# The order of work in the slots of a selective scan, and what feeds and follows it: decays, dt's chain, gates, start values

## The chip, the cores and the metric

The kernel runs on one core of a Trainium2 chip, in float32. The metric is the device time of one execution in microseconds (us). A core has TensorE (PE, matmuls into the eight banks of PSUM), VectorE (DVE), ScalarE (ACT), GpSimd (POOL) and SyncE (SP, which here issues nearly all DMAs); each runs its own queue of instructions in order.

## The reference, cut to what matters

The network has four layers, each an attention-like block and a feed-forward block with a residual and a layer norm, on two sequences of 1024 tokens and 1024 channels. The change touches one block, the selective state space block of layer 2:

```python
def step(h, inp):
    x_t, dt_t, B_t, C_t = inp
    dA = jnp.exp(dt_t[..., None] * A)
    dBx = dt_t[..., None] * B_t[:, None, :] * x_t[..., None]
    h = dA * h + dBx
    y = jnp.einsum('bdn,bn->bd', h, C_t)
    return (h, y)
```

There are 2048 inner channels d and 16 states n. x is a projection of the input after a causal convolution of four taps and a silu; dt, B and C are projections of x, each normed, and dt goes through a second projection and a softplus. y gets D times x added, is multiplied by silu(z), where z is the second half of the input projection (the gate), and goes through an output projection.

## The kernel before, in words

`net_kernel` takes the two sequences one after the other; `l2_attn` computes the block for one of them. The 1024 tokens are two halves (u = 0, 1) of 512, the 2048 channels 16 chunks (c) of 128. A scan over 512 tokens is one VectorE instruction whose 128 partitions hold 8 channels times 16 states. So a half takes 256 scans, two to a slot: 128 slots (SL), 8 to a chunk, 256 slots for a sequence. The slot number k runs through both halves; `of(k)` gives half, chunk and place.

The order of everything in this stage is written out by hand in a loop over slots from k = -23 (BEFORE) to 261, inside `manual_schedule`. In a slot stand, in this order of issue:

- `rows(k + 6)` (L1273): SP loads dt times x for 8 channels, spread over the 16 states, from the DRAM tensor dxd into one of nine buffers h (512 KB);
- `times_b(k + 2)` (L1279): POOL multiplies h by B;
- `keep(k - 1)` (L1304): in u = 0, ScalarE copies the last column of the scans of the slot before into hst, from where the half u = 1 starts;
- one PE call of other work; then for m = 0, 1: `scan(k, m)` (L1296) on VectorE and `decay(k + 1, m)`: a PE matmul (L1286) that spreads dt from the tile hl into a PSUM bank, and ScalarE's exponential in place (L1288). In u = 1 `decay` also adds decay times hst into h's first column (L1291, a column operation of 128x1);
- between the two: the work that is due in this slot (`late`, filled by `at(k, f)`), and the second PE call;
- `states(k - 2)` in odd slots: PE sums over states into a bank py (L1316, L1318), one bank for a chunk;
- `times_c(k - 1)` (L1307): VectorE multiplies h by C, which lies in PSUM;
- in slots with k % 8 == 4: `y_out` is put down for eight slots later. It copies py with ScalarE (L1332), multiplies it by the gate with POOL (L1333), and stores it to yd (L1334).

The other PE calls are the projections of x for u = 1 (`ins`, with `l2_x` on ScalarE, `l2_taps` on VectorE, L1124, and `l2_silu` a slot apart each), of z (`gates`), of dt, B and C (`xproj`, then `l2_norm` and `l2_spread`), and the output projection of u = 0 (`outs`, L1441). All take their banks from one pool of eight (`ps`).

`l2_dt` starts a chunk's dt 16 slots before its first scan: a matmul, then ScalarE's softplus in pieces (`act1`, `act2`), sums and the product with x on POOL (`pool1`, `sum1`, `times_x`), four writes to dxd (L1240), the split of dt into hl and lo (`parts`, `rest`) and two transfers that put lo into hl (L1258; `send`). x comes back from the DRAM tensor xcd into xi (L1520). The steps' slots, counted from `l2_dt`, are given in a list:

```python
for n, f in ((1, act1), (2, act2), (3, pool1), (4, sum1), (5, times_x), (7, parts), (7, rest), (8, send)):
    at(k + n, f)
```

Of the kernel before, what the change touches and what calls it, by code (L numbers as in the profile page):

```python
# [27 lines left out]
class Net:  # L28
# [1032 lines left out]
    def l2_attn(self, b, ready, last):  # L1061
# [4 lines left out]
        with (  # L1066
# [56 lines left out]
                for k in range(1, 4):  # L1123
                    nc.vector.scalar_tensor_tensor(p, xp[:, k : k + HALF], cw[:, c, k : k + 1], p, ALU.mult, ALU.add)  # L1124

            def l2_silu(u, c, p):
                acc = tmp("xo")
                self.other = True
                nc.scalar.activation(acc, p, AF.Silu)
                nc.sync.dma_start(xcd[u][c][:], acc)  # L1130
                return acc

            def l2_px(u, c, acc):
# [24 lines left out]
                    elif c % 4 < 3:  # L1158
                        quarter[-1](c % 4 - 1)

            def l2_norm(u):

                raw = tmp("xo")
                nc.scalar.copy(raw[:NF, :], px.pop(u)[:NF, :])
                p = self.ps()
                for tt in range(4):
                    nc.tensor.transpose(
                        p[:, tt * NF : (tt + 1) * NF], raw[:NF, tt * P : (tt + 1) * P], self.ident[:NF, :NF]
                    )
                pn = tmp("pn", 1, 4 * NF)  # L1170
                nc.scalar.activation(pn, p[:, : 4 * NF], AF.Square)
                ss = self.small([P, 4, 3], "ss")
                parts = ((0, NR), (NR, N), (NR + N, N))
                pnv, pv = [t.rearrange("p (t f) -> p t f", f=NF) for t in (pn, p[:, : 4 * NF])]
                for j, (lo, n) in enumerate(parts):
                    nc.vector.tensor_reduce(ss[:, :, j], pnv[:, :, lo : lo + n], AX.X, ALU.add)
                nc.vector.tensor_scalar(ss[:, :, 0:1], ss[:, :, 0:1], 1.0 / NR, 1e-6, ALU.mult, ALU.add)
                nc.vector.tensor_scalar(ss[:, :, 1:3], ss[:, :, 1:3], 1.0 / N, 1e-6, ALU.mult, ALU.add)
                rr = self.small([P, 4, 3], "rr")
                self.rsqrt(rr, ss)  # L1180
                for tt in range(4):
                    for j, (lo, n) in enumerate(parts):
                        nc.vector.scalar_tensor_tensor(
                            pnv[:, tt, lo : lo + n], pv[:, tt, lo : lo + n], rr[:, tt, j : j + 1],
                            lnw[:, lo : lo + n], ALU.mult, ALU.mult,
                        )
                return pnv
# [20 lines left out]
            def l2_dt(u, c, k):  # L1208

                p = self.ps()  # L1210
                nc.tensor.matmul(
                    p, wd[c // 8][: NF + 1, (c % 8) * P : (c % 8 + 1) * P], norms[u][0], start=True, stop=True
                )
                xs[u, c] = xc = tmp("xi")
                at(k + 3, nc.sync.dma_start, xc, xcd[u][c][:])
                e, one, lg = tmp("e", 1), tmp("one", 1), tmp("lg", 1)
                dt, dtx = lg, e
                rl = tmp("rl", 1)

                def act1():  # L1220
                    nc.scalar.activation(rl, p, AF.Relu)
                    nc.scalar.activation(e, p, AF.Abs)
                    nc.scalar.activation(e, e, AF.Exp, scale=-1.0)

                def act2():
                    nc.scalar.activation(one, e, AF.Identity, bias=self.one)
                    nc.scalar.activation(lg, one, AF.Ln)
                    nc.scalar.activation(one, one, AF.Identity, bias=neg)

                def pool1():  # L1230
                    nc.gpsimd.tensor_tensor(e, e, one, ALU.subtract)
                    nc.gpsimd.tensor_tensor(lg, lg, e, ALU.add)

                def sum1():
                    nc.gpsimd.tensor_tensor(dt, lg, rl, ALU.add)

                def times_x():
                    nc.gpsimd.tensor_tensor(dtx, dt, xc, ALU.mult)
                    for j in range(4):
                        nc.sync.dma_start(dxd[u][c][:, j, :], dtx[32 * j : 32 * j + 32, :])  # L1240

                low = [None]

                def parts():

                    hl[u, c] = tp.tile([P, 2, HALF], R, tag="hl", bufs=2, name=self.nm("hl"))
                    nc.scalar.copy(hl[u, c], dt.unsqueeze(1).to_broadcast([P, 2, HALF]))

                def rest():

                    lo = low[0] = tp.tile([P, HALF], R, tag="lo", bufs=1, name=self.nm("lo"))
                    nc.gpsimd.tensor_tensor(lo, dt, hl[u, c][:, 0, :].bitcast(F), ALU.subtract)

                def send():

                    lo = low[0]
                    for j in range(2):
                        nc.sync.dma_start(  # L1258
                            hl[u, c][64 - 64 * j : P - 64 * j, j, :].bitcast(F), lo[64 * j : 64 * j + 64, :].bitcast(F)
                        )  # L1260

                for n, f in ((1, act1), (2, act2), (3, pool1), (4, sum1), (5, times_x), (7, parts), (7, rest), (8, send)):
                    at(k + n, f)


# [17 lines left out]
            def decay(k, m):  # L1283
                u, c, q, jj = of(k)
                dA[k, m] = self.ps()
                nc.tensor.matmul(dA[k, m], rep[:, 4 * m + q, :], hl[u, c][:, jj, :], start=True, stop=True)  # L1286
                g = 16 * c + 4 * q + 2 * jj + m
                nc.scalar.activation(dA[k, m], dA[k, m], AF.Exp, scale=A[:, g : g + 1])  # L1288
                if u:
                    h0 = hs[k][:, m, 0:1]  # L1290
                    nc.scalar.activation(h0, dA[k, m][:, 0:1], AF.Identity, scale=hst[:, g : g + 1], bias=h0)  # L1291

            def scan(k, m):
                u, c, q, jj = of(k)
                g = 16 * c + 4 * q + 2 * jj + m
                nc.vector.tensor_tensor_scan(  # L1296
                    hs[k][:, m, :], dA.pop((k, m)), hs[k][:, m, :], 0.0, ALU.mult, ALU.add
                )

            def keep(k):  # L1300
# [27 lines left out]
            def y_out(k):  # L1328
                u, c = k // SL, k % SL // 8
                sz = zt.pop((u, c))  # L1330
                yo = tmp("one", 1)
                nc.scalar.copy(yo, py.pop((u, c)))  # L1332
                nc.gpsimd.tensor_tensor(sz, sz, yo, ALU.mult)  # L1333
                nc.sync.dma_start(yd[u][c][:], sz)  # L1334

            def ins(u):

                def one(u, c):
# [6 lines left out]
                    def call(k, now):  # L1345
                        if k == 0:
                            w["p"] = self.ps()
                        p = w["p"]
                        nc.tensor.matmul(  # L1349
                            p, w["w"][:, k * P : (k + 1) * P], self.xcols(k, u0, HALF), start=k == 0, stop=k == KD - 1  # L1350
                        )
                        if k == KD - 1:
                            def x():
                                w["x"] = l2_x(u, c, p)
                            at(now + 1, x)
                            at(now + 2, lambda: l2_taps(c, p, w["x"]))

                            def s():
                                w["s"] = l2_silu(u, c, p)
                                silu_z()  # L1360
                            at(now + 3, s)
                    return load, [(call, k) for k in range(KD)]
# [2 lines left out]
            def xproj(u):  # L1365

                def one(c2):
# [7 lines left out]
                    def call(n, now):  # L1375
                        l2_px(u, 2 * c2 + n, w["x"][:, n * HALF : (n + 1) * HALF])
                        if 2 * c2 + n == NCH - 1:
                            at(now + 1, lambda: at(now + 3, l2_spread, u, l2_norm(u)))
                    return load, [(call, n) for n in range(2)]
                return [one(c2) for c2 in range(NCH // 2)]  # L1380

# [80 lines left out]
            with self.tc.manual_schedule():  # L1462
# [12 lines left out]
                take(xproj(1), 4)  # L1475
                take(z0[12:] + z1[:6], 20)
                taken = 0
                at(-BEFORE, lambda: at(4 - BEFORE, l2_spread, 0, l2_norm(0)))
                for k in range(-BEFORE, 2 * SL + 6):
                    if -16 <= k < 2 * SL - 16 and k % 8 == 0:  # L1480
                        l2_dt((k + 16) // SL, (k + 16) % SL // 8, k)
# [26 lines left out]
                        times_b(k + 2)  # L1508
                    if 0 <= k - 1 < 2 * SL:
                        keep(k - 1)  # L1510
                    pe()
                    for m in range(2):
                        if live:
                            scan(k, m)
                        if 0 <= k + 1 < 2 * SL:
                            decay(k + 1, m)
                        if m:
                            break
                        for f, args in late.pop(k, []):
                            f(*args)  # L1520
                        pe(True)
                    if k % 2 == 1 and 0 <= k - 2 < 2 * SL:
                        states(k - 2)
                    if 0 <= k - 1 < 2 * SL:
                        times_c(k - 1)
                    if live and k % 8 == 4:
                        at(k + 8, y_out, k)
                    if live and k % 8 == 0:
                        skip(k // SL, k % SL // 8)
                while late:  # L1530
# [462 lines left out]
```

## Time and profile before

| | |
|---|---|
| time, median of 3 runs | 5128.9 us (5122.4 to 5136.8) |
| the profiled execution's own time | 5130.3 us |
| its span, first to last instruction | 5128.4 us |
| granted TensorE clock, mean | 0.968 |
| busy share PE, DVE, ACT, POOL | 92%, 61%, 41%, 41% |
| scans L1296 | 1024, 1207 ns each |
| products with C, L1307 | 512, 1193 ns each |
| products with B, L1279 (POOL) | 512, 2367 ns each |
| exponentials L1288 (ACT) | 1024, 657 ns each |
| column operations L1291 (ACT) | 512, 352 ns each |
| first and last scan, first sequence | 1052.1 to 2003.4 us |
| first and last scan, second sequence | 3601.9 to 4545.4 us |

The profile is of one execution. A row of a group gives line, engine, operation, output<-inputs, sizes, count, then busy time and the mean of one in ns, then the time that the engine sat idle before it and who ended that. Row "DVE h L1296 <- ACT h L1291" of the waits reads: VectorE sat idle before L1296 until ScalarE's L1291 was done; the numbers are us in all, times, longest. In a table by stretch each engine has its busy time and, in brackets, its instructions; PEclk is the granted clock, DMA share the mean busy share of the 16 DMA engines.

### The profile page before, as it was taken

Reading aid. Unit: us, or ns where it says so; the run is one execution under the profiler, and the core shown is the slowest. Engines: PE = TensorE matmul, PEld = TensorE weight load, DVE = VectorE, ACT = ScalarE, POOL = GpSimd, SP = SyncE. Lnnn points to the kernel's source line nnn. Section 1 sums busy time; section 2 is a strip of 40 time slices with the busy share of each in tenths; the row PEclk is TensorE's granted clock in tenths of the full one; section 3 lists DMA queues with packets and bytes.
Section 4 is the critical chain, followed back from the end, with each engine's and each line's share of the span. In section 5 each row is a group of like instructions: output and inputs, shape, how many; then the busy total and the mean of one; then the engine's idle time right before and its main releaser. Section 6 shows DMA issues by size and latency. Waiting matters only on the chain. (4 is left out here: it accounts for less than half of the span.)

```text
span 5128.4 us, 50257 instructions
## 1 busy us (share of the span) xinstructions
PE 4706.3 (92%) x16584; PEld 2237.2 (44%) x16584; DVE 3128.0 (61%) x4322; ACT 2109.7 (41%) x4485; POOL 2097.7 (41%) x1259
## 2 busy tenths in 40 slices
PE   8989989998897888999999999899888988899999
PEld 3347645433332333455433576554333333344544
DVE  5453256389999997225365422652899999963153
ACT  2431232377677774001024311424776777720010
POOL 2013121078798885100020220200887998831010
PEclk9999999999999999999999999999999999999999
DMA  2144212388889998201111432113888899971100
GB/s 88 36 159 143 97 48 81 131 216 217 220 225 242 236 244 226 90 33 46 49 67 38 173 119 89 54 51 103 220 219 224 214 247 245 249 210 65 55 20 33
DMA packets 254871, 708.06 MB, mean 138 GB/s; under 512 B 37008, under 2 KB 54544, under 8 KB 254612
## 3 DMA queue, kind: packets, MB, share of 16 engines
q1 hardware_dynamic: 248340, 683.88, 46.7%
q0 software_dynamic: 6272, 20.98, 1.2%
q8 instruction: 133, 2.18, 0.2%
q14 instruction: 126, 1.03, 0.1%
HBM read 599.60 MB, written 86.25 MB: 134 GB/s over the span
## 5 line engine op out<-in xcount | busy, mean ns | idle before, releaser
L1296 DVE TENSOR_TENSOR_SCAN h<-ps,h 128x512 f32<-128x512 f32 x1024 | 1204.1, 1207 | 88.9 <-ACT h L1291 47.2
L1279 POOL TENSOR_TENSOR h<-h,br 128x1024 f32<-128x1024 f32 x512 | 1201.0, 2367 | 43.3 <-DMA h<-dxd 20.7
L1286 PE MATMUL ps<-hl,rep 128*128 128x512 f32 x1024 | 717.9, 708 | 119.9 <-DVE h L1296 94.7
L1288 ACT ACTIVATE ps<-ps,l_Alog 128x512 f32<-128x512 f32 x1024 | 667.9, 657 | 216.9 <-PE ps L1286 213.6
L1307 DVE TENSOR_TENSOR h<-h,ps 128x1024 f32<-128x1024 f32 x512 | 610.8, 1193 | 0.0
L1403 PE MATMUL ps<-xT,w 128*128 128x512 f32 x1024 | 541.1, 615 | 10.2 <-DVE h L1296 7.9
L1608 POOL TENSOR_TENSOR x<-x,row 128x1024 f32<-128x1024 f32 x48 | 112.3, 2349 | 796.0 <-PE ps L130 796.0
L1286 PEld LDWEIGHTS ps<-hl,rep 128*128 128x128 f32 x1024 | 198.6, 195 | 523.6 <-DVE h L1296 340.1
L152 DVE TENSOR_TENSOR x<-x,ps 128x512 f32<-128x512 f32 x192 | 128.4, 681 | 434.4 <-PE ps L1785 145.6
L1318 PE MATMUL ps<-h,sel 128*32 128x512 f32 x2048 | 365.1, 638 | 18.8 <-DVE h L1307 18.2
L104 PE MATMUL ps<-xT,w 128*128 128x512 f32 x768 | 336.1, 592 | 0.0
L177 ACT ACTIVATE rs<-mv 128x1 f32<-128x1 f32 (+2 forms) x88 | 17.9, 203 | 705.7 <-DVE mv L171 705.4
L1441 PE MATMUL ps<-w,w 128*128 128x512 f32 x512 | 279.9, 630 | 20.8 <-DMA w<-yd 12.1
L1403 PEld LDWEIGHTS ps<-xT,w 128*128 128x128 f32 x1024 | 190.6, 195 | 204.2 <-issue 136.7
L104 PE MATMUL ps<-w,xT 128*128 128x512 f32 (+1 forms) x768 | 278.3, 522 | 0.0
L1124 DVE SCALAR_TENSOR_TENSOR ps<-xp,l_convw,ps 128x512 f32<-128x512 f32 x192 | 144.4, 752 | 213.4 <-ACT ps L1119 208.9
L767 POOL TENSOR_TENSOR s<-s,l1r 128x512 f32<-128x512 f32 x64 | 66.5, 1040 | 487.7 <-DVE l1r L766 481.8
L1349 PE MATMUL ps<-xT,w 128*128 128x512 f32 x512 | 251.9, 602 | 0.7
L1291 ACT ACTIVATE h<-ps,h,hst 128x1 f32<-128x1 f32 x512 | 180.0, 352 | 118.5 <-POOL h L1279 93.9
L1782 PE MATMUL ps<-w,xT 128*128 128x512 f32 x512 | 227.4, 597 | 0.0
L1622 PE MATMUL ps<-w,w 128*128 128x512 f32 x512 | 222.6, 594 | 4.2 <-DMA w<-yd 4.2
L104 PEld LDWEIGHTS ps<-xT,w 128*128 128x128 f32 x768 | 144.8, 189 | 183.4 <-issue 177.6
(289 smaller groups left out, 7319.9 us busy)
## 6 DMA issues: line engine op xcount, KB each, us to landing
h<-dxd SPq DMA_DIRECT2D x512, 512.0 KB, 7.2
w<-l_in SPq DMA_DIRECT2D x128, 512.0 KB, 6.7
w<-l_out SPq DMA_DIRECT2D x96, 512.0 KB, 6.2
w<-l_conv SPq DMA_DIRECT2D x54, 512.0 KB, 3.9
w<-cvd SPq DMA_DIRECT2D x36, 512.0 KB, 3.3
w<-l_fw SPq DMA_DIRECT2D x32, 512.0 KB, 4.4
xcd<-xo SPq DMA_DIRECT2D x64, 256.0 KB, 2.2
xi<-xcd SPq DMA_DIRECT2D x64, 256.0 KB, 5.4
```

The costliest lines, as they stand in the source:

```text
L104: self.nc.tensor.matmul(out, lhsT, rhs, start=j == 0, stop=j == n - 1)
L1279: nc.gpsimd.tensor_tensor(hs[k], hs[k], norms[of(k)[0]][1].unsqueeze(1).to_broadcast([P, 2, HALF]), ALU.mult)
L1286: nc.tensor.matmul(dA[k, m], rep[:, 4 * m + q, :], hl[u, c][:, jj, :], start=True, stop=True)
L1288: nc.scalar.activation(dA[k, m], dA[k, m], AF.Exp, scale=A[:, g : g + 1])
L1296: nc.vector.tensor_tensor_scan(hs[k][:, m, :], dA.pop((k, m)), hs[k][:, m, :], 0.0, ALU.mult, ALU.add)
L1307: nc.vector.tensor_tensor(hs[k], hs[k], norms[of(k)[0]][3].unsqueeze(1).to_broadcast([P, 2, HALF]), ALU.mult)
L1318: nc.tensor.matmul(py[u, c][32 * j : 32 * j + 32, :], self.sel[:, q, :], hs[k - 1 + j // 2][:, j % 2, :], start=False, stop=q == 3,)
L1349: nc.tensor.matmul(p, w["w"][:, k * P : (k + 1) * P], self.xcols(k, u0, HALF), start=k == 0, stop=k == KD - 1)
L1403: nc.tensor.matmul(p, w["w"][:, k * P : (k + 1) * P], self.xcols(k, u * HALF, HALF), start=k == 0, stop=k == KD - 1)
L1441: nc.tensor.matmul(p, y[:, cc, t * P : (t + 1) * P], wt[:, cc * HALF : (cc + 1) * HALF], start=c2 == 0 and cc == 0, stop=last,)
L1622: nc.tensor.matmul(acc[tt], y[:, cc * HALF + tt * P : cc * HALF + (tt + 1) * P], w[:, cc * HALF : (cc + 1) * HALF], start=c == 0, stop=c = ...
L1782: nc.tensor.matmul(p, self.xcols(k, tt * P, P), wt[k][:, ns], start=k == 0, stop=False)
```

## The change

- The due work of a slot (`late`) comes ahead of the first PE call and of both scans.
- After `scan(k, 0)` comes `decay(k + 1, 1)`, after `scan(k, 1)` comes `decay(k + 2, 0)`: each decay stands one scan sooner in the order.
- The column operation is gone from `decay`; `scan` takes its initial value from hst in u = 1.
- `y_out` comes six slots after it is put down, not eight, and multiplies on VectorE, straight from py; the store to yd is issued a slot later.
- dt's chain has one step of an engine in a slot and is longer; the product with x uses the tile `one`, not `e`; the writes to dxd and the product with x are apart.
- `l2_silu` of u = 1 stores its result a slot later. `l2_norm` is cut in two, a slot apart, and `l2_spread` comes a slot later for u = 1.

```diff
-            def l2_silu(u, c, p):
+            def l2_silu(u, c, p, now=0):
...
-                nc.sync.dma_start(xcd[u][c][:], acc)
+                if u:
+                    at(now + 1, nc.sync.dma_start, xcd[u][c][:], acc)
+                else:
+                    nc.sync.dma_start(xcd[u][c][:], acc)
...
-            def l2_norm(u):
+            def l2_norm1(u):
...
                 nc.scalar.activation(pn, p[:, : 4 * NF], AF.Square)
+                return p, pn
+
+            def l2_norm(u, p, pn):
...
-                at(k + 3, nc.sync.dma_start, xc, xcd[u][c][:])
+                at(k + 4, nc.sync.dma_start, xc, xcd[u][c][:])
...
-                dt, dtx = lg, e
+                dt, dtx = lg, one
...
                 def act1():
                     nc.scalar.activation(rl, p, AF.Relu)
                     nc.scalar.activation(e, p, AF.Abs)
+
+                def act2():
                     nc.scalar.activation(e, e, AF.Exp, scale=-1.0)
 
-                def act2():
+                def act3():
                     nc.scalar.activation(one, e, AF.Identity, bias=self.one)
+
+                def act4():
                     nc.scalar.activation(lg, one, AF.Ln)
+
+                def act5():
                     nc.scalar.activation(one, one, AF.Identity, bias=neg)
 
                 def pool1():
                     nc.gpsimd.tensor_tensor(e, e, one, ALU.subtract)
+
+                def pool2():
                     nc.gpsimd.tensor_tensor(lg, lg, e, ALU.add)
...
                 def times_x():
                     nc.gpsimd.tensor_tensor(dtx, dt, xc, ALU.mult)
+
+                def send_x():
                     for j in range(4):
                         nc.sync.dma_start(dxd[u][c][:, j, :], dtx[32 * j : 32 * j + 32, :])
...
-                for n, f in ((1, act1), (2, act2), (3, pool1), (4, sum1), (5, times_x), (7, parts), (7, rest), (8, send)):
+                for n, f in (
+                    (1, act1), (2, act2), (3, act3), (4, act4), (5, act5), (5, pool1), (6, pool2), (7, sum1),
+                    (8, times_x), (8, parts), (9, send_x), (9, rest), (10, send),
+                ):
                     at(k + n, f)
...
                 nc.scalar.activation(dA[k, m], dA[k, m], AF.Exp, scale=A[:, g : g + 1])
-                if u:
-                    h0 = hs[k][:, m, 0:1]
-                    nc.scalar.activation(h0, dA[k, m][:, 0:1], AF.Identity, scale=hst[:, g : g + 1], bias=h0)
...
-                    hs[k][:, m, :], dA.pop((k, m)), hs[k][:, m, :], 0.0, ALU.mult, ALU.add
+                    hs[k][:, m, :], dA.pop((k, m)), hs[k][:, m, :], hst[:, g : g + 1] if u else 0.0, ALU.mult, ALU.add
...
                 sz = zt.pop((u, c))
-                yo = tmp("one", 1)
-                nc.scalar.copy(yo, py.pop((u, c)))
-                nc.gpsimd.tensor_tensor(sz, sz, yo, ALU.mult)
-                nc.sync.dma_start(yd[u][c][:], sz)
+                nc.vector.tensor_tensor(sz, sz, py.pop((u, c)), ALU.mult)
+                at(k + 7, nc.sync.dma_start, yd[u][c][:], sz)
...
                     if 0 <= k - 1 < 2 * SL:
                         keep(k - 1)
+                    for f, args in late.pop(k, []):
+                        f(*args)
                     pe()
                     for m in range(2):
                         if live:
                             scan(k, m)
-                        if 0 <= k + 1 < 2 * SL:
-                            decay(k + 1, m)
+                        if 0 <= k + 1 + m < 2 * SL:
+                            decay(k + 1 + m, 1 - m)
                         if m:
                             break
-                        for f, args in late.pop(k, []):
-                            f(*args)
                         pe(True)
...
                     if live and k % 8 == 4:
-                        at(k + 8, y_out, k)
+                        at(k + 6, y_out, k)
```

More of the change, by code (lines that the diff above doesn't have):

```diff
@@ L1358, in s @@
                             def s():
-                                w["s"] = l2_silu(u, c, p)
+                                w["s"] = l2_silu(u, c, p, now + 3)
                                 silu_z()
@@ L1377, in call @@
                         if 2 * c2 + n == NCH - 1:
-                            at(now + 1, lambda: at(now + 3, l2_spread, u, l2_norm(u)))
+                            at(now + 1, lambda: w.update(n=l2_norm1(u)))
+                            at(now + 2, lambda: at(now + 4, l2_spread, u, l2_norm(u, *w["n"])))
                     return load, [(call, n) for n in range(2)]
@@ L1477, in l2_attn @@
                 taken = 0
-                at(-BEFORE, lambda: at(4 - BEFORE, l2_spread, 0, l2_norm(0)))
+                at(-BEFORE, lambda: at(4 - BEFORE, l2_spread, 0, l2_norm(0, *l2_norm1(0))))
                 for k in range(-BEFORE, 2 * SL + 6):
```

## The prediction

> **What bounds the kernel now.** I read the page first (slices, groups), then busy time by stretch, then what VectorE waits for in each stretch, then single slots. The scans are two stages, slices 8 to 15 and 28 to 35, one for each sequence. I cut each at the slot where its second half (u = 1) begins.
>
> ```profile
> span 5128.4 us, 50257 instructions
> ...
> DVE  5453256389999997225365422652899999963153
> ...
> POOL 2013121078798885100020220200887998831010
> ```
>
> ```profile
> core 0: us, PE busy (x) PEld busy (x) DVE busy (x) ACT busy (x) POOL busy (x), PEclk, DMA share, GB/s
> 1052.00:1536.40 484.40, 428.78 (x1341) 162.80 (x1339) 462.92 (x438) 345.03 (x659) 418.91 (x226) 0.97 0.84 220
> 1536.40:2003.40 467.00, 395.33 (x1241) 147.64 (x1239) 440.18 (x398) 339.46 (x674) 399.58 (x212) 0.95 0.93 240
> 3601.80:4084.20 482.40, 429.21 (x1342) 163.18 (x1340) 463.10 (x437) 345.00 (x659) 419.04 (x226) 0.97 0.83 220
> 4084.20:4545.50 461.30, 395.99 (x1240) 146.71 (x1238) 439.69 (x398) 339.56 (x674) 399.70 (x212) 0.95 0.93 244
> ```
>
> VectorE is busy 94 to 96% of all four stretches; no other compute engine is. So a scan stage lasts as long as VectorE's work plus VectorE's idle time: 21.5 + 26.8 + 19.3 + 21.6 = 89 us in all. That is the most the change can save inside the stages. Who causes it, from the waits of VectorE in the first sequence's stage:
>
> ```profile
> engine line waited for: us in total, times, longest us
> DVE h L1296 <- ACT h L1291: 26.1, 33, 2.3
> DVE h L1296 <- ACT ps L1288: 13.2, 14, 2.3
> ```
>
> The first is all of u = 1, the second all in u = 0; the second sequence has 21.1 and 18.1. Both are ScalarE being late: with the exponential of a decay (L1288), or with the column operation behind it (L1291). An undisturbed slot is two scans and one product:
>
> ```profile
> 1440.01 2.33 DVE L1296 TENSOR_TENSOR_SCAN h<-ps,h 128x512 f32<-128x512 f32 x2
> 1442.25 1.19 DVE L1307 TENSOR_TENSOR h<-h,ps 128x1024 f32<-128x1024 f32 x1
> 1443.37 2.33 DVE L1296 TENSOR_TENSOR_SCAN h<-ps,h 128x512 f32<-128x512 f32 x2
> ```
>
> It takes 3.36 us, though the three durations (1.207 twice, 1.193) add to 3.61: each instruction starts 82 ns before the one ahead ends. So an added VectorE instruction costs its duration less about 0.08 us.
>
> **The change, part by part.**
>
> *Gate on VectorE.* Removed, 64 times: ScalarE's copy L1332 (0.58 us) and POOL's product L1333 (1.27). Added, 64 times: one VectorE product of an SBUF and a PSUM operand. Nearest row is L982, the same form: 685 ns, 605 net. 62 lie inside the scans, where nothing covers them: **+37 us**. On POOL eight slots cost 8 x 2.37 + 6 x 1.27 = 26.6 us before, against VectorE's 26.9; after, 25.3.
>
> *No column operation.* Removed, 512 times: L1291 on ScalarE (352 ns, 180 us in all), which also made ScalarE wait for POOL's product (93.9 us over the run). Added: the scan of u = 1 takes its initial value from a column of hst. No row shows a scan with one. Rows of like shape with and without a per-partition scalar:
>
> ```profile
> L1723 DVE SCALAR_TENSOR_TENSOR x<-ps,rinv,x 128x512 f32<-128x512 f32 x32 | 22.9, 746 | 9.0 <-PE ps L104 8.7 <-issue 0.3
> ...
> L628 DVE SCALAR_TENSOR_TENSOR qkv<-cf,ps 128x512 f32<-128x512 f32 x22 | 15.1, 686 | 69.4 <-PE ps L612 69.4
> ```
>
> 60 ns more. Bounds: nothing, if the scan loads its start under other work, and 66 ns (L1124 against L628); a gain is excluded, since the form only adds a read. I take 60: 512 x 0.06 = **+31 us**.
>
> A rule speaks against this part. Rows inside the scans:
>
> ```profile
> L1124 DVE SCALAR_TENSOR_TENSOR ps<-xp,l_convw,ps 128x512 f32<-128x512 f32 x33 | 24.6, 747 | 2.0 <-ACT ps L1119 1.2
> ...
> L181 DVE TENSOR_TENSOR rsq<-rsq,ss 128x12 f32<-128x12 f32 x1 | 2.3, 2261 | 0.0
> ```
>
> L181, tiny, takes 2261 ns here. The Trainium skill (SBUF — State Buffer, "Who interferes with whom") says why: a VectorE instruction with two SBUF inputs shares a read port with GpSimd, and one waits out the other. If the column counted as a second SBUF input beside h, each of the 512 scans could wait about 1 us (half a POOL product): some +500 us. But L1124 reads xp and its scalar from SBUF, and keeps 747 ns with POOL at 86%. I take the row: no lock. The gate reads one SBUF and one PSUM operand, as L982.
>
> *Decays half a slot sooner, due work first.* No instruction added. Decay n is now issued after scan n-3 instead of n-2, and ScalarE does a slot's due work before both exponentials instead of between them. Check on a stall of before: in slots 12, 28, ... ScalarE runs, from the end of a scan, keep 0.19, exp 0.66, gate copy 0.58, table load 1.28, silus 0.60 + 2 x 0.62, table load 1.28, exp 0.66 = 6.5 us; the second exp is due after 1.12 + 3.36 + 1.13 = 5.6. Short by 0.9; the trace has 1.11 at five slots. After: keep 0.19, Ln 0.63, the same 4.4, exp 0.66 = 5.9: short by 0.3. An extra PSUM bank is held by decays; the gate, read at slot 10 of a chunk instead of 12, gives one back before the next accumulator is taken. Counting tiles in program order, a decay's bank was freed 3 to 4 scans earlier before, 4 to 5 after.
>
> *dt's chain.* Same instructions, one ScalarE or POOL step a slot. It goes from step 5 to step 9 for the four dxd writes, 8 to 10 for the two hl writes, 3 to 4 for the xi load; the y write goes a slot after its product, and the xcd writes of u = 1 a slot after the silu. All go through SP; POOL issues no DMA in these stages. SP no longer stands waiting for POOL (L1240 85.1 us, L1334 73.6 in the first sequence), and POOL no longer for xi (17.1). Several u = 1 stalls (1.97 and 2.28 us at chunk starts) go back to that late xi load. What tightens is the dxd write against the first row load (a rival below).
>
> *Sum.* Idle 89 us goes. What is late next: in u = 0 the silu slot (5 x 0.4), the norm and the start, about 4.5 a sequence; in u = 1 row loads and out-projection weights at a DMA share of 0.93, about 5.5; so 20 us remain. Before and after the stages: the first decay one half slot sooner in PE's queue, and the last gate without its 1.86 us of copy and POOL product, about -3 a sequence. -89 + 20 + 37 + 31 - 6 = **-7 us** on the profiled execution's 5130.3 (span 5128.4). That execution is 1.4 above the median, 5128.9, of the three runs; on the median the sum gives 5122, and I say 5124, as PE's wait at the gate (next) is not quite nothing.
>
> Bounds of the gate's own wait: the product stands first in VectorE's queue at slot 10 and needs PE's last state sums of slot 9, and both scans are queued behind it. In the trace those sums end mostly 0.6 to 2.2 us before that slot, and twice after it; they move behind one more decay. Zero to 1.1 us (one scan) each: 0 to 70 us. I take 2 in all, since the decay's bank is free four scans back.
>
> **The rivals.**
>
> *The scan's start is free.* For: a scan takes 1133 ns from start to start, against 605 for a product of as many elements, so one more read may hide in it. Against: both scalar forms pay. 5124 - 31 = 5093.
>
> *Slack not bought.* ScalarE's late work is as long as before; if half of the 89 us stays, 5124 + 24 = 5148. Against: ScalarE loses 108 us of work per sequence.
>
> *The row loads come late (slower).* Before, dxd was written five steps before the first row load of its chunk. Now it is one. SP comes to the write in an odd slot, behind a row load that waits for that slot's state sums (2.4 us), issues four (1.7), and the next row load stands in SP until they land (median 2.9, longest 9.4). It goes 7 us into slot 9 instead of 2. Then landing (median 8.5 in u = 1, longest 14.3) and POOL's 2.4: 18 of the 24.4 us to its scan. Cover is 6 us at the medians; it decides when both landings together pass 17.5 us, against 11.4. hl, queued behind, lands at about 17. If half of the 32 chunks of u = 1 lose 2.3 us, +37: 5161. For it: DMA share 0.93. Against: the total traffic is the same, and SP's other waits go.
>
> **How the numbers follow.** Main case 0.46, 5124, own range 5106 to 5142. Free start 0.22; slack not bought 0.15; late rows 0.17. Within 0.3% (15 us), which is about what a measurement of this kernel can tell from no change, lie most of the main case and a third of the slack case. Faster: 0.25 of the main case and nearly all of the free start, 0.33. Slower: nearly all of the late rows, two thirds of the slack case, a little of the main, 0.27. Same: 0.40. The range runs from the free start with all stalls gone (5086) to the late rows (5163).
>
> **What would show it.** Right: VectorE's waits in the scans about 20 us in all, no L1291; 64 gate products near 0.68 us and with hardly a wait; scans of u = 1 near 1.27 us, those of u = 0 unchanged; u = 0 stretches 6 to 10 us shorter, u = 1 within 8 us of before. Wrong: u = 1 scans at 1.21 (then 5093); waits of POOL's product on h<-dxd in every chunk, or SP's L1273 on dxd for over 5 us each (then 5161); gate products that wait for PE.

## The result: 0.8% slower, and the profile after

The changed kernel takes 5170.0 us (median of 4 runs, 5165.4 to 5173.5) where the kernel before takes 5129.6 in the same comparison: a ratio of 1.0081, with a 95% interval of 1.0065 to 1.0097. The profiled execution has a span of 5164.2 us, 35.8 more than before. The prediction was 5124, with a range that ended at 5163: it was wrong, in sign and in size.

First the slices of the page after: nothing has changed its bound. VectorE is the full engine of slices 8 to 15 and 28 to 35, as before.

```profile
span 5164.2 us, 49160 instructions
...
DVE  5452266389999997215365422652999999962153
...
POOL 2023020078797874100010320201887978731010
```

Then the table by stretch, cut at the same places (first scan, first scan of u = 1, last scan, for each sequence).

```profile
core 0: us, PE busy (x) PEld busy (x) DVE busy (x) ACT busy (x) POOL busy (x), PEclk, DMA share, GB/s
1054.80:1532.30 477.50, 422.29 (x1333) 161.88 (x1332) 465.97 (x450) 329.21 (x637) 396.11 (x209) 0.96 0.83 219
1532.30:2012.90 480.60, 402.32 (x1238) 145.91 (x1238) 462.30 (x414) 251.53 (x402) 381.24 (x198) 0.93 0.88 238
3618.20:4099.00 480.80, 422.46 (x1333) 162.57 (x1332) 465.50 (x451) 329.29 (x637) 396.00 (x209) 0.96 0.83 217
4099.00:4583.00 484.00, 404.33 (x1238) 146.53 (x1238) 462.41 (x414) 251.22 (x402) 381.38 (x198) 0.92 0.88 236
```

The stretches of u = 0 are 6.9 and 1.6 us shorter than before, those of u = 1 are 13.6 and 22.7 us longer. In all the stages grew by 28 us: VectorE's work by 50.3, while its idle time (length less busy) fell from 89.0 to 66.7, so by 22.3 only. The remaining 7.9 us lie outside the stages. There, each first scan stands 4.2 us farther behind its norm than before (66.0 us instead of 61.8), because the taps (L1124) of slot 0, and the ScalarE step that they wait for, are now ahead of it:

```profile
1052.58 2.34 DVE L1124 SCALAR_TENSOR_TENSOR ps<-xp,l_convw,ps 128x512 f32<-128x512 f32 x3 [7.67 <-ACT ps L1119]
...
1054.83 3.45 DVE L1313 TENSOR_TENSOR_SCAN h<-ps,h 128x512 f32<-128x512 f32 x3
```

What each instruction costs is as predicted. Three rows of the page's groups: scans of u = 1, scans of u = 0, POOL's product with B; then two of the gate products by tile (shortest, median and longest in ns; `row` and `zo` are two places in which z is kept).

```profile
L1313 DVE TENSOR_TENSOR_SCAN h<-ps,hst,h 128x512 f32<-128x512 f32 x512 | 628.9, 1267 | 26.1 <-ACT ps L1308 26.1
L1313 DVE TENSOR_TENSOR_SCAN h<-ps,h 128x512 f32<-128x512 f32 x512 | 598.5, 1207 | 14.9 <-ACT ps L1308 14.9
L1299 POOL TENSOR_TENSOR h<-h,br 128x1024 f32<-128x1024 f32 x512 | 1205.1, 2368 | 131.7 <-DMA h<-dxd 91.0
```

```profile
L1348 DVE TENSOR_TENSOR row<-row,ps x32: 676/681/690, 1088.4 to 4534.1; 128x512 f32<-128x512 f32 x32
L1348 DVE TENSOR_TENSOR zo<-zo,ps x32: 669/686/689, 1148.3 to 4588.1; 128x512 f32<-128x512 f32 x32
```

The scan with a start value costs 60 ns more, the gate product 0.68 us. What is not as predicted is in the waits. The lines of VectorE and ScalarE in the first sequence's stage (total us, times, longest):

```profile
engine line waited for: us in total, times, longest us
ACT ps L1308 <- PE ps L1306: 212.9, 227, 4.3
...
ACT one L1235 <- DMA dxd<-one: 99.5, 29, 10.2
...
DVE h L1313 <- ACT ps L1308: 17.2, 15, 5.6
...
DVE zo L1348 <- PE ps L1335: 6.5, 9, 1.2
...
DVE row L1348 <- PE ps L1335: 3.8, 3, 2.0
```

Two kinds are new. ScalarE stands 29 times, for 99.5 us, at L1235 (`act3`, 1 + e) until a DMA has *read* the tile `one`: the trace of before shows no such wait of ScalarE. And VectorE waits 12 times at the gate for PE's state sums; over both stages the gate's waits are 19.2 us, and scans wait 41.0 us for an exponential (L1308).

One of the long waits, from the timeline (start, duration, engine and line, idle before it in brackets; lines between left out):

```profile
1630.74 3.77 SPq L1257 DMA_DIRECT2D dxd<-one  x4
...
1640.30 0.72 ACT L1235 ACTIVATE one<-e,one 128x512 f32<-128x512 f32 x1 [10.18 <-DMA dxd<-one]
...
1640.92 1.22 ACT L1308 ACTIVATE ps<-ps,l_Alog 128x512 f32<-128x512 f32 x2
1641.60 1.28 DVE L1313 TENSOR_TENSOR_SCAN h<-ps,hst,h 128x512 f32<-128x512 f32 x1 [5.63 <-ACT ps L1308]
```

The four writes of dt times x to dxd are issued from 1630.7 us on; ScalarE may overwrite `one` for the next chunk only when they have landed, at 1640.3. The exponentials of two decays stand behind it in ScalarE's queue, and the scan that needs the first is 5.63 us late.

It follows from the list of steps. dt times x now lives in `one`, of which there is one buffer. It is written to dxd at step 9, and the next chunk, eight slots behind, writes `one` at its step 3, which is step 11: two slots, 6.7 us at 3.36 us a slot, for an issue and a landing that here took 9.6. Before, dt times x lived in `e`, written to dxd at step 5 and overwritten by the next chunk at step 9: four slots, 13.4 us, and ScalarE did not wait for it.

### The profile page after: what moved, and what is told of

The parts are those of the page before. It is cut to its first block, busy times and chain, and to the rows that moved or that the text cites. A ratio compares the mean times of both kernels' runs of the same rounds, so it can differ in the third digit from the quotient of the medians.

```text
span 5164.2 us, 49160 instructions
## 1 busy us (share of the span) xinstructions
PE 4712.2 (91%) x16584; PEld 2233.8 (43%) x16584; DVE 3180.9 (62%) x4386; ACT 1908.1 (37%) x3909; POOL 2017.0 (39%) x1195
## 5 line engine op out<-in xcount | busy, mean ns | idle before, releaser
L1306 PE MATMUL ps<-hl,rep 128*128 128x512 f32 x1024 | 713.2, 701 | 163.5 <-DVE h L1313 147.3
L1308 ACT ACTIVATE ps<-ps,l_Alog 128x512 f32<-128x512 f32 x1024 | 657.6, 660 | 437.6 <-PE ps L1306 435.7
L1313 DVE TENSOR_TENSOR_SCAN h<-ps,hst,h 128x512 f32<-128x512 f32 x512 | 628.9, 1267 | 26.1 <-ACT ps L1308 26.1
L1324 DVE TENSOR_TENSOR h<-h,ps 128x1024 f32<-128x1024 f32 x512 | 611.9, 1195 | 0.4 <-ACT hst L1321 0.4
L1313 DVE TENSOR_TENSOR_SCAN h<-ps,h 128x512 f32<-128x512 f32 x512 | 598.5, 1207 | 14.9 <-ACT ps L1308 14.9
L1419 PE MATMUL ps<-xT,w 128*128 128x512 f32 x1024 | 544.8, 619 | 13.7 <-DVE h L1313 13.2
L1306 PEld LDWEIGHTS ps<-hl,rep 128*128 128x128 f32 x1024 | 199.3, 196 | 594.1 <-DVE h L1313 428.5
L1335 PE MATMUL ps<-h,sel 128*32 128x512 f32 x2048 | 347.4, 665 | 7.2 <-DVE h L1324 7.2
L1124 DVE SCALAR_TENSOR_TENSOR ps<-xp,l_convw,ps 128x512 f32<-128x512 f32 x192 | 145.0, 755 | 226.5 <-ACT ps L1119 222.0
L1457 PE MATMUL ps<-w,w 128*128 128x512 f32 x512 | 277.5, 626 | 5.9 <-DVE h L1313 4.5
L1419 PEld LDWEIGHTS ps<-xT,w 128*128 128x128 f32 x1024 | 191.5, 195 | 209.7 <-issue 139.6
L1244 POOL TENSOR_TENSOR e<-e,one 128x512 f32<-128x512 f32 x64 | 81.5, 1273 | 474.3 <-ACT one L1241 471.5
```

The source lines that it names most:

```text
L1313: nc.vector.tensor_tensor_scan(hs[k][:, m, :], dA.pop((k, m)), hs[k][:, m, :], hst[:, g : g + 1] if u else 0.0, ALU.mult, ALU.add)
L1324: nc.vector.tensor_tensor(hs[k], hs[k], norms[of(k)[0]][3].unsqueeze(1).to_broadcast([P, 2, HALF]), ALU.mult)
L1335: nc.tensor.matmul(py[u, c][32 * j : 32 * j + 32, :], self.sel[:, q, :], hs[k - 1 + j // 2][:, j % 2, :], start=False, stop=q == 3,)
L1419: nc.tensor.matmul(p, w["w"][:, k * P : (k + 1) * P], self.xcols(k, u * HALF, HALF), start=k == 0, stop=k == KD - 1)
L1457: nc.tensor.matmul(p, y[:, cc, t * P : (t + 1) * P], wt[:, cc * HALF : (cc + 1) * HALF], start=c2 == 0 and cc == 0, stop=last,)
```

## The experiments

The theory after this reading: the tile `one` makes ScalarE wait, which makes exponentials late and is the first cost; the gate's wait for PE is the second. The rivals were the late row loads of the prediction (POOL's wait on h<-dxd is 91.0 us over the run where it was 20.7), and the added work itself, which is all there if the stalls merely move. Each kernel is compared with the kernel before on its own chip (medians of before 5128.0 to 5133.1), so the ratios are what is compared between kernels.

| kernel | median us | ratio to before, 95% | idle of VectorE in both stages, us |
|---|---|---|---|
| before | 5129.6 | | 89.0 |
| changed | 5170.0 | 1.0081 (1.0065 to 1.0097) | 66.7 |
| own_tile | 5141.8 | 1.0030 (1.0018 to 1.0041) | 41.1 |
| gate_back | 5135.3 | 1.0015 (1.0008 to 1.0022) | 73.2 |
| column_back | 5151.9 | 1.0051 (1.0038 to 1.0064) | 74.5 |
| chain_back | 5157.0 | 1.0057 (1.0044 to 1.0070) | 40.9 |
| own_gate_end | 5139.8 | 1.0015 (1.0004 to 1.0025) | 31.7 |
| own_gate | 5112.2 | 0.9960 (0.9945 to 0.9974) | 42.6 |
| own_gate_column | 5109.1 | 0.9955 (0.9942 to 0.9968) | 64.6 |
| own_gate_column_2 | 5108.6 | 0.9951 (0.9936 to 0.9966) | 65.9 |
| order_only | 5133.7 | 1.0008 (0.9996 to 1.0020) | 87.4 |
| chain_only | 5109.3 | 0.9955 (0.9940 to 0.9970) | 66.5 |

**own_tile: the changed kernel, with a tile of its own for dt times x.**

```diff
-                dt, dtx = lg, one
+                dt, dtx = lg, tmp("dx", 1)
```

> The changed kernel, but dt times x gets a tile of its own instead of the tile one. Theory T (a tile): in the changed kernel ScalarE's first step on one (1 + e) waits for the dxd write of the chunk before, which still reads one: 99.5 us of ScalarE waiting in the first sequence, and behind it stand the exponentials; VectorE's stalls at slots with k % 8 == 4 (some 30 us in both sequences) go, so about 5140 us. Theory R (rows): the loss is the row loads that stand in SP until the dxd write has landed; that stays as it is, so no change, 5170 us.

The ratio falls from 1.0081 to 1.0030. ScalarE's wait at L1235 is gone, scans wait 11.3 us for exponentials instead of 41.0, and the gate's waits stay (21.0). From the waits of the first sequence's stage:

```profile
DVE zo L1348 <- PE ps L1335: 6.9, 8, 2.1
...
DVE h L1313 <- ACT ps L1308: 4.8, 6, 1.5
...
DVE row L1348 <- PE ps L1335: 1.8, 4, 0.5
```

The row loads are as late as ever, by the page's row of POOL's product:

```profile
L1299 POOL TENSOR_TENSOR h<-h,br 128x1024 f32<-128x1024 f32 x512 | 1204.6, 2367 | 151.6 <-DMA h<-dxd 96.0
```

POOL waits 96.0 us for them, more than in the changed kernel, and this costs VectorE 0.8 us in both stages. So the tile was the cause of 0.51%, some 26 us, and the late rows of next to nothing: VectorE hardly waits for POOL's product, however late its rows are.

**gate_back: the changed kernel with the gate on ScalarE and POOL, at its new slot.** The copy gets a tile of its own.

```diff
-                nc.vector.tensor_tensor(sz, sz, py.pop((u, c)), ALU.mult)
+                yo = tmp("yo", 1)
+                nc.scalar.copy(yo, py.pop((u, c)))
+                nc.gpsimd.tensor_tensor(sz, sz, yo, ALU.mult)
```

> The changed kernel, but the gate is again ScalarE's copy and POOL's product (with a tile of its own), at the changed slot. Theory G: the gate on VectorE costs 62 x 0.60 = 37 us of work and 19 us of waiting for PE's state sums, all on the bound engine: about 5114 us. Rival: VectorE's 19 us of waiting only stand in for stalls that come anyway a little later (exponentials late by the same PE work): about 5133 us. If ScalarE and POOL have no room for it: 5160 us or more.

VectorE gets its 37 us of work back and loses its 19 us of gate waits, but its idle time rises to 73.2: ScalarE, still stopped by `one`, now has the copy too, and waits for the state sums in VectorE's place. The waits of the first sequence:

```profile
ACT one L1235 <- DMA dxd<-one: 93.1, 26, 9.7
...
DVE h L1313 <- ACT ps L1308: 30.8, 17, 6.3
...
ACT yo L1349 <- PE ps L1335: 19.4, 25, 9.8
```

The gain, 0.66% or 34 us, is the removed work. So the 19 us of gate waits were not a cost by themselves while `one` stopped ScalarE: they moved.

**column_back: the changed kernel with the column operation back on ScalarE.**

```diff
+                if u:
+                    h0 = hs[k][:, m, 0:1]
+                    nc.scalar.activation(h0, dA[k, m][:, 0:1], AF.Identity, scale=hst[:, g : g + 1], bias=h0)
...
-                    hs[k][:, m, :], dA.pop((k, m)), hs[k][:, m, :], hst[:, g : g + 1] if u else 0.0, ALU.mult, ALU.add
+                    hs[k][:, m, :], dA.pop((k, m)), hs[k][:, m, :], 0.0, ALU.mult, ALU.add
```

> The changed kernel, but the column operation on ScalarE is back and the scans of u = 1 start from 0. Theory: a start value costs a scan 60 ns, 512 scans, so 31 us go: about 5139 us, scans of u = 1 back at 1207 ns. Rival: ScalarE gets 180 us of work back, and each column operation waits for POOL's product, so its stalls come back too (47 us of VectorE waiting before): about 5155 to 5175 us.

It gains 0.30% (15 us). The 31 us of the start value go, and waits for the column operation come, 19.1 us in the first sequence and 22.5 in the second.

**chain_back: the changed kernel with dt's chain at the steps of before,** dt times x in `e` again.

```diff
-                at(k + 4, nc.sync.dma_start, xc, xcd[u][c][:])
+                at(k + 3, nc.sync.dma_start, xc, xcd[u][c][:])
-                dt, dtx = lg, one
+                dt, dtx = lg, e
...
-                    (1, act1), (2, act2), (3, act3), (4, act4), (5, act5), (5, pool1), (6, pool2), (7, sum1),
-                    (8, times_x), (8, parts), (9, send_x), (9, rest), (10, send),
+                    (1, act1), (1, act2), (2, act3), (2, act4), (2, act5), (3, pool1), (3, pool2), (4, sum1),
+                    (5, times_x), (5, send_x), (7, parts), (7, rest), (8, send),
```

> The changed kernel, but dt's chain in its old steps (three ScalarE steps in one slot, dt times x at step 5 into e, hl at step 8, xi load at step 3). Theory T and theory R both expect the loss of the late dxd write to go (30 us or more), less what ScalarE's clumps cost (0.5 us a chunk at most, under 15 us): 5140 to 5155 us. If it stays near 5170 us, the chain is not where the time went.

VectorE's idle time is that of own_tile (40.9), which shows the tile from the other side: take it out of the wait either way, and 26 us of idle go. But the time falls only 0.24%, half as much. In the profile u = 0 has 4 and 7 us more of VectorE's work than own_tile's, and this is four operations of the norm, 12 numbers wide (L180 to L183): in the two sequences they take 13.8 us here and 2.6 in own_tile. The long ones end with a product of POOL:

```profile
1394.02 4.65 POOL L1299 TENSOR_TENSOR h<-h,br 128x1024 f32<-128x1024 f32 x2
1394.20 2.20 DVE L181 TENSOR_TENSOR rsq<-rsq,ss 128x12 f32<-128x12 f32 x1
1396.43 2.27 DVE L182 TENSOR_SCALAR rsq<-rsq 128x12 f32<-128x12 f32 x1
```

The two products end at 1396.37 and 1398.67, L181 and L182 at 1396.40 and 1398.70. So 11 of the some 14 us by which this kernel is slower than own_tile are the norm's. In the kernel before these operations took 11.0 us, in the changed kernel 2.5: it depends on where they fall among POOL's products, which the change did not look at.

**own_gate_end: own_tile with the gate product at the end of slot 10,** behind both scans and the product with C.

```diff
-                    if live and k % 8 == 4:
-                        at(k + 6, y_out, k)
+                    if k % 8 == 2 and 0 <= k - 6 < 2 * SL:
+                        y_out(k - 6)
```

> As the changed kernel with dt times x in its own tile (5142), and the gate product on VectorE at the end of slot 10 of a chunk, behind both scans and the product with C, instead of at its start. Theory W: VectorE's 21 us of waiting at the gate for PE's last state sums go, the 37 us of work stay: about 5121 us. Rival: those waits only move to the scans behind (VectorE runs ahead into exponentials that PE's same lateness holds up): 5135 us or more.

The gate waits for PE no more. All of VectorE's waits in the first sequence's stage over 1 us in total:

```profile
DVE h L1313 <- ACT ps L1308: 10.7, 14, 2.1
...
DVE rsq L180 <- ACT rr L178: 2.0, 1, 2.0
```

Of the 21.0 us of gate waits in own_tile, about half come back, mostly as waits for exponentials (21.4 us in both stages, 11.3 in own_tile); idle falls by 9.4, and from the norms to the last scans the profile is 9.5 us shorter. The ratio falls by 0.15% (8 us); the two intervals overlap.

**own_gate: own_tile and gate_back together.** To make room in SBUF, the norm's squares go into a tile that was there.

```diff
-                pn = tmp("pn", 1, 4 * NF)
+                pn = tmp("xo")[:, : 4 * NF]
```

> The changed kernel with both: dt times x in its own tile, and the gate back on ScalarE and POOL. If the two losses are separate, 5142 - 35 = about 5107 us, VectorE's idle time in the scans under 30 us. Rival: with the gate's copy ScalarE waits for PE in its queue ahead of the exponentials, so the waits return there: about 5125 us.

0.9960: this kernel is faster than the one before. Against gate_back, which has the same gate, the tile of its own is worth 0.55% here. With ScalarE no longer stopped, its copy and POOL's product cost no stall: idle 42.6 us against own_tile's 41.1.

**own_gate_column: own_gate, and the column operation back.** Its edit is that of column_back.

> As the kernel before it in this list, with the column operation back too. What is left of the change is the order of decays and due work and dt's chain. Adding what each part gave alone: 5170 - 28 - 35 - 18 = about 5089 us, and VectorE's work as in the kernel before the change. Rival: ScalarE has all its old work again, its stalls come back as they were before (89 us of idle): about 5125 us.

> The same kernel as own_gate_column, once more, on the chip of chain_only, so that the two can be told apart on one chip: 5105 to 5114 by every theory.

0.9955, and 0.9951 on another chip: the same as own_gate within the intervals, where some 18 us less were expected. The page's rows of the scans and of the column operation say why:

```profile
L1316 DVE TENSOR_TENSOR_SCAN h<-ps,h 128x512 f32<-128x512 f32 x1024 | 1198.6, 1205 | 55.9 <-ACT h L1311 43.1
...
L1311 ACT ACTIVATE h<-ps,h,hst 128x1 f32<-128x1 f32 x512 | 180.1, 352 | 109.8 <-POOL h L1299 86.0
```

VectorE's busy time in the stages falls by 27 us from own_gate and its idle time rises by 22, nearly all of it waits for L1311 (43.1 us), which itself waits for POOL. A start value at 60 ns a scan and a column operation with its stalls cost about the same.

**order_only: the kernel before with the order alone** (due work first, decays a scan sooner).

```diff
+                    for f, args in late.pop(k, []):
+                        f(*args)
                     pe()
...
-                        if 0 <= k + 1 < 2 * SL:
-                            decay(k + 1, m)
+                        if 0 <= k + 1 + m < 2 * SL:
+                            decay(k + 1 + m, 1 - m)
                         if m:
                             break
-                        for f, args in late.pop(k, []):
-                            f(*args)
```

> The kernel before, with two edits of the change alone: decays one scan sooner, due work ahead of the scans. Theory: ScalarE's stalls of before (39 us with its exponentials or column operations behind due work in each u, 89 us idle in all) shrink by a third to a half: 5085 to 5100 us. Rival: the exponentials hang on PSUM banks that scans free, so the order buys nothing without the other parts: 5120 to 5130 us.

1.0008 with an interval across 1: in the time of the kernel, the order buys nothing by itself. The waits of the first sequence:

```profile
ACT h L1291 <- POOL h L1279: 74.9, 43, 6.8
...
DVE h L1296 <- ACT h L1291: 29.2, 28, 3.4
...
DVE h L1296 <- ACT ps L1288: 8.5, 11, 2.1
```

u = 0 waits less for exponentials (8.5 us, 13.2 before), u = 1 a little more for the column (29.2, 26.1 before): the column operation waits for POOL's product, and a decay that is done sooner does not bring that.

That nothing is gained is a balance. In the profile the two stages are some 15 us shorter than before, nearly all of it VectorE's work: 9.6 us are the norm's narrow operations (1.4 us instead of 11.0), 4 us taps that moved ahead of the first scans. The rest of the profile is some 19 us longer: each first scan stands 5.2 us farther behind its norm, and from the last scan of the first sequence to the second norm it takes 8.1 us more, at a lower clock of TensorE (last section).

**chain_only: own_gate_column with the order of before,** the reverse of the diff above on it.

> As own_gate_column, but with the order of before: due work between the two scans, each decay after the scan of the same place. Left of the change are dt's longer chain with the product of dt and x in a tile of its own, the split norm and the later stores; gate and column operation are those of before (the gate at slot 10). Against order_only (5134, stalls of 87 us) and own_gate_column (5109). Theory: the order was worth nothing by itself because ScalarE's chain steps came in lumps behind which the exponentials stood; with the chain spread, ScalarE's column operation is what still stalls u = 1, and that wants the decays sooner, so order and chain need each other: 5120 to 5132 here. Rival: the chain with its own tile is the whole gain and the order is worth nothing in either company: 5105 to 5113.

0.9955, the ratio of own_gate_column. So the order has no part in the gain with the chain either. (Here too the stages are some 12 us longer without the new order than in own_gate_column_2, and the medians are the same.) Table by stretch:

```profile
1054.90:1532.00 477.10, 429.99 (x1341) 162.52 (x1339) 464.74 (x438) 337.50 (x659) 416.18 (x225) 0.98 0.84 220
1532.00:1987.60 455.60, 397.32 (x1243) 149.03 (x1241) 437.67 (x398) 336.80 (x674) 402.74 (x215) 0.95 0.94 251
3591.10:4068.00 476.90, 432.39 (x1341) 162.96 (x1339) 464.62 (x437) 337.30 (x658) 416.96 (x226) 0.97 0.85 220
4068.00:4530.40 462.40, 400.43 (x1243) 149.68 (x1242) 438.48 (x398) 337.35 (x674) 401.78 (x214) 0.94 0.93 248
```

VectorE's work is that of before (1805.5 us against 1805.9), its idle time 22.5 us less, the stages 23.1 us shorter, and 0.45% of the time is 23 us (in the two profiled executions 7.7 of the 23.1 come back outside the stages). This kernel is the one before plus the spread chain with its own tile, the norm in two steps, the later stores, and the copy of the gate two slots sooner and in a tile of its own, where before it shared `one` with the chain. Which of these carries the 23 us was not separated; by the waits in the stages, exponentials have 8.9 us of it, the column operation 5.6, and the norm's wait for its squares 5.4. chain_only and own_gate_column are the fastest of all these kernels.

## Why the prediction was wrong

The step that failed is the term "20 us remain" of the sum: 66.7 us of idle remained. With it the sum reads -89 + 67 + 37 + 31 - 6 = +40, against +35.8 of the profiled spans. That this is near is in part luck: work in the stages was 18 us less than the sum has, and what lies outside them 14 us more (measured: -22 + 50 + 8). Point by point:

- *dt's chain.* The text said that "what tightens is the dxd write against the first row load". It followed each step within its own chunk, down to the scan that needs it, and not from one chunk to the next: that the product moved into `one`, and that `one` is written again two slots after it is sent. This is the larger part of the miss: own_tile takes 29.7 us of waits for exponentials and 25.6 us of idle time away, and 0.51% of the time.
- *The gate's own wait.* The bounds were 0 to 1.1 us each, the value taken 2 us in all, "since the decay's bank is free four scans back". It was 21.4 us at 25 of the 64 gates, 19.2 of it inside the stages, up to 2.1 each. One of the longest, in the timeline of the changed kernel:

```profile
1928.89 1.20 DVE L1324 TENSOR_TENSOR h<-h,ps 128x1024 f32<-128x1024 f32 x1
...
1931.33 0.79 PE L1306 MATMUL ps<-hl,rep 128*128 128x512 f32 x1 [1.18 <-DVE h L1313]
...
1931.93 1.91 PE L1419 MATMUL ps<-xT,w 128*128 128x512 f32 x2
...
1932.37 1.20 DVE L1324 TENSOR_TENSOR h<-h,ps 128x1024 f32<-128x1024 f32 x1
1932.85 1.42 PE L1306 MATMUL ps<-hl,rep 128*128 128x512 f32 x1
...
1934.19 1.28 PE L1335 MATMUL ps<-h,sel 128*32 128x512 f32 x8
...
1935.57 0.69 DVE L1348 TENSOR_TENSOR row<-row,ps 128x512 f32<-128x512 f32 x1 [2.01 <-PE ps L1335]
```

  The last input of the state sums is there at 1930.1 (L1324, the product with C of slot 7 of the chunk). But ahead of the sums in PE's queue stand two decays (L1306) and two matmuls of another projection (L1419); the first decay waits for a scan until 1931.33, and the sums end near 1935.5, while VectorE has been free since 1933.57. So the reason failed too: decays did wait for scans, and over the run more than before. The two pages, before and after:

```profile
L1286 PE MATMUL ps<-hl,rep 128*128 128x512 f32 x1024 | 717.9, 708 | 119.9 <-DVE h L1296 94.7
...
L1306 PE MATMUL ps<-hl,rep 128*128 128x512 f32 x1024 | 713.2, 701 | 163.5 <-DVE h L1313 147.3
```

  own_gate_end, with the gate two scans and a product later, has no such wait at the gate, and 9.4 us less idle time. What remains there, 31.7 us, is still 12 more than the sum's 20, mostly exponentials that come late (21.4); what makes these late was not traced.

- *Decays sooner, due work first.* The check of one kind of stall in u = 0 was right in direction: in the first sequence 13.2 us of these waits became 8.5 in order_only. That the change would clear 69 of the 89 us was not. u = 1's stalls came from POOL through the column operation, and what ended them in the changed kernel was the start value, at 31 us. (Of the second sequence's 18.1 us of waits for exponentials, 5.7 lie ahead of its first scan and so were not among the 89.)
- *Work.* The prices were right, 60 ns a scan and 0.68 us a gate less an overlap of 0.08; the sum of 68 was not, with 50.3 us measured inside the stages. Three things make up most of the difference. Instructions overlap more: starts ahead of the end of the instruction before add up to 132 us, 12 more than before, and the sum has 5 of these in the price of the gates. The taps of slot 0, 4 us, moved ahead of the stages. And the norm's four narrow operations, which the sum did not look at, took 2.5 us instead of 11.0.
- *The shared read port.* The row was the right guide: the scans with h and a column of hst in SBUF have a mean of 1267 ns while POOL is busy 79% of u = 1, so the column does not make them wait for POOL, and does not count as a second input under the rule that was weighed (the Trainium skill, SBUF — State Buffer, "Who interferes with whom"). For two whole inputs the trace agrees with the rule: L181, which reads two tiles in SBUF, ends with POOL's product in chain_back's lines above (L182, which reads one, does so too).
- *Before and after the stages.* -6 was predicted, +7.9 came, the wrong way. The sum did not see that the due work of slot 0 now stands ahead of the first scan, which costs 4.2 us a sequence; chain_only, with the order of before, has its first scans as soon after the norm as the kernel before.
- *The rivals.* The free start is out: the start costs 60 ns. Slack not bought was the nearest in mechanism (5148, half of the 89 us stays; it was three quarters, at other places than it said). The late rows, at 5161 nearest in number, came true up to POOL (waits on h<-dxd in the first sequence 26 times, 41.4 us) and stopped there, and SP's row loads stood 85.0 us for the writes to dxd there, 2.8 each and not over 5; that 5161 is near 5170 is luck.
- *The signs named.* L1291 gone, gates at 0.68, scans at 1.27, u = 0 shorter: right, though by 6.9 and 1.6 instead of 6 to 10. Waits of about 20 us, u = 1 within 8 us: wrong. "Gate products that wait for PE" was named as what would make it wrong, and did.

## What to carry to other kernels

When a chain of steps is stretched over more slots than the period at which it starts anew, list for every single-buffered tile its last reader, DMAs included, and the slot in which the next round writes it; a DMA that still reads it stops an engine that executes in order, with all that is queued behind. A buffer of its own for the value that is sent brought back 0.51% of the 0.81% here, at the cost of one tile. And when work goes to the engine that bounds a stage to cure a wait (by the sum, 68 us of work for 69 us of waits), try first what else the wait hangs on: the version with the spread chain and ScalarE's gate and column operation (chain_only) gained 23 us without any work added to VectorE.

## What the runs showed of the hardware

The granted TensorE clock went with the order of issue, which I had not expected. Its mean over the two scan stages is 0.962 and 0.958 in the kernel before, 0.963 and 0.958 in chain_only, which has the same order; in the ten other profiles, all with the new order, it is 0.935 to 0.952. The clocks of whole executions say the same: on one chip 0.964 to 0.970 in 23 of the kernel before against 0.958 to 0.964 in 12 of order_only, on another 0.967 to 0.969 in 6 of chain_only against 0.960 to 0.967 in 11 of own_gate_column_2; in each pair the order is the difference. VectorE's scans from a start of 0 keep their 1.205 to 1.208 us at either.

Outside, where PE bounds, the time goes with the clock. From the last scan of the first sequence to the second norm, where all but the last gate is the same code, the kernel before takes 1536.8 us at a mean clock of 0.976, own_gate 1546.0 at 0.970: the product of time and clock is 1499.9 and 1499.6, and in all twelve profiles between 1499 and 1506. The windows show it, with the same matmuls to within two:

```profile
2003.40:3540.00 1536.60, 1461.48 (x5571) 778.58 (x5572) 629.94 (x1275) 331.45 (x851) 206.17 (x173) 0.98 0.23 79
```

```profile
1984.50:3530.50 1546.00, 1470.38 (x5569) 782.17 (x5570) 626.54 (x1275) 332.22 (x852) 207.01 (x173) 0.97 0.23 77
```

So own_gate, whose scan stages are 31 us shorter than before, gave 9 us back there. What lowers the clock behind the stages stays open: the changed kernel, with the new order and long stages, has 0.977 between them; order_only, with the new order and short ones, 0.970.
